# Turning attention weights by VectorE and transfers within SBUF in place of TensorE, in a stack of four graph layers

## The chip, the cores and the metric

The kernel runs on one core of one Trainium2 chip. The metric is the device time of one execution, in microseconds. Profiles are of one execution each.

Names used below: PE is TensorE, DVE is VectorE, ACT is ScalarE, POOL is GpSimd, SP is SyncE, whose queue issues all transfers. SBUF is the working memory of 128 partitions, and PSUM the memory that PE writes to.

## The reference

The input is 32 graphs of 512 nodes with 256 channels, and one adjacency matrix of 512x512 for all. Four layers follow each other; each is a graph attention whose output is added to its input and normalised. All is float32.

```python
# --- layer 0: one head of 256, additive
h = x @ W;  s1 = h @ a1;  s2 = h @ a2
e = leaky_relu(s1[:, :, None] + s2[:, None, :], 0.2)
att = softmax(where(adj > 0, e, NEG));  x = layernorm(x + elu(att @ h))
# --- layer 1: a transformer block, eight heads of 32, with softmax((q k^T)/sqrt(32)) masked, two
#     layer norms and a feed-forward part of 256; then x = layernorm(x + block(x))
# --- layer 2: four heads of 64, additive as layer 0, head by head; elu
# --- layer 3: e = leaky_relu((x W1) (x W2)^T), masked softmax, att @ (x W3), relu
```

The weights `att` of a head are computed with the query in the partition (128 queries a block, 512 keys in the row). The product `att @ h` sums over keys, and PE sums over partitions, so every block of weights has to be turned first.

## The kernel before

**Names.** The layers are called a (layer 0), b, c and d. `B` is 32 graphs, `N` 512 nodes, `P` 128, `NB` 4 blocks of 128 nodes, `F` 2 halves of a graph, `FB` 2 blocks in a half. `Gat` (L716) is the class for a and c, `Transformer` (L814) for b, `Bilinear` (L951) for d.

**The steps of an additive head** (`Gat.attend`, L741). PE spreads the target's score over all partitions as a row of 512 (L755). For each of four blocks, DVE adds the mask, writes a tile `t` of 128x512 and takes the row's maximum (`masked`, L637). ACT applies the leaky slope (L666) and the exponential with the sum of the row (L672), in place. Then `turn` (L543) turns each block: four PE transposes of 128x128 into one PSUM bank (L549), and a copy of 128x512 from the bank into the tile `pT`, on ACT (L492) or DVE (L494). Layer c multiplies two heads at a time by `weighted` (L554, matmuls L561), with the values as the stationary operand; layer a uses `rows_weighted` (L801, matmuls L807), with the turned weights as the stationary operand. `scaled` (L580) divides by the sums. Layers b and d use the same `turn`; b's scores come from L853, its mask and minimum from L867, its exponential from L874; d's scores come from L975.

**Counts.** A graph has 16 turned blocks in layer c, 4 in a, 32 in b and 4 in d, or 1792 blocks and 7168 transposes in all.

**Buffers.** A tile `t` is 2 KB a partition and there are 18; a `pT` holds half a graph's turned weights of one head, 4 KB, and there are 8. PSUM has 8 banks.

**What sets the order.** The program is a list of operations, each with the engines it may run on and a cost in microseconds (`Plan.op`, L107). `Plan.order` (L140) plays this list with these costs. At each free engine it picks the ready operation with the lowest key, made of the graph's number times `AGE`, the remaining path, and a table `URGENT` by engine and stage; up to `WINDOW` = 4 graphs are open at once. It also assigns every buffer slot and, where an operation may run on ACT or DVE (`copied`, L487), the engine. Its result is written out as a fixed order for each engine (L1062). At run time the engines keep that order and wait for each other by semaphores. SP's queue holds the loads of `x` and of its transpose (L340) and the stores (L1041), in that order too. The tables `AGE`, `URGENT` and `SWITCH_WEIGHT` are numbers written into the file.

Of the kernel before, what the change touches and what calls it, by code (L numbers as in the profile page):

```python
# [11 lines left out]
I32 = mybir.dt.int32  # L12
# [15 lines left out]
BUFS = dict(t=18, pT=8, x=6, xT=3, v=5, qk=4, y=5, e=2, n=2, nT=2, hT=2, oT=4, small=8)  # L28
# [11 lines left out]
AGE = {"PE": 51, "ACT": 138, "DVE": -107, "POOL": 461, "SP": 20}  # L40
URGENT = {
    "PE": {"a0": -417, "a1": 491, "a2": -867, "b0": -448, "b1": 197, "b2": 839, "c0": -557, "c1": -258, "c2": 203, "d0": -909, "d1": -511, "d2": -1186, "a3": 1287, "a4": 1218, "b3": -47, "b4": 169, "c3": 2234, "c4": 712},
    "ACT": {"a0": -671, "a1": 422, "a2": 770, "b0": 459, "b1": 253, "b2": 93, "c0": 729, "c1": 136, "c2": -360, "d0": 573, "d1": -523, "d2": -1234, "a3": 806, "a4": -162, "b3": 370, "b4": 340, "c3": 698, "c4": -390},
    "DVE": {"a0": -247, "a1": 1195, "a2": 496, "b0": 1368, "b1": 273, "b2": -132, "c0": -1160, "c1": 19, "c2": 666, "d0": -845, "d1": -1056, "d2": -1458, "a3": 1297, "a4": 438, "b3": -527, "b4": 175, "c3": 138, "c4": 1482},
    "POOL": {"a0": -896, "a1": -817, "a2": 582, "b0": 3, "b1": -713, "b2": 227, "c0": -148, "c1": -607, "c2": 1624, "d0": 582, "d1": 1022, "d2": -1512, "a3": -446, "a4": 431, "b3": 270, "b4": 1342, "c3": 708, "c4": 734},
    "SP": {},
# [6 lines left out]
SWITCH_WEIGHT = 661  # L53
# [45 lines left out]
class Plan:  # L99
# [7 lines left out]
    def op(self, where, issue, writes=(), reads=(), takes=(), lag=0.0, port=False, form="full"):  # L107
# [10 lines left out]
        for buf in takes:  # L118
            if not buf.users and buf.tag is not None:
                o.takes.append(buf)  # L120
                self.bufs.append(buf)
                buf.users.append(o)
# [170 lines left out]
def gnn_stack(  # L293
# [83 lines left out]
    def attention_weights(w, w_sb, a, H, D, name):  # L377
# [3 lines left out]
        for which, lo in enumerate((0, D)):  # L381
            av = buf("t", [P, D], f"{name}_a{which}")
            on_all(a[lo : lo + D], av)
            for k in range(NC):
                prod = buf("t", [P, H, D], f"{name}_prod{which}{k}")
# [14 lines left out]
    def mask():  # L400
        for i in range(NB):
            adj_sb = buf("t", [P, N], f"adj{i}", dtype=I32)
            load(adj_sb, lambda adj_sb=adj_sb: adj_sb[:], adj[block(i)])

            def issue(e, i=i, adj_sb=adj_sb):
                nc.vector.tensor_scalar(neg[:, i], adj_sb[:], 0.0, NEG, ALU.is_le, ALU.mult)

            op({DVE: 0.4}, issue, [(neg, i)], [adj_sb])

    def feed_forward_weights():  # L410


        b2_sb = buf("t", [P, C], "b2_sb")
# [32 lines left out]
    def bilinear_weights():  # L446
# [3 lines left out]
        for w, name in ((wa, "wa"), (wb, "wb")):  # L450
            w_sb = buf("t", [P, NC, C], f"{name}_sb")
            by_chunk(w, w_sb)
            wT = buf("t", [P, NC, C], f"{name}T", NC)
# [89 lines left out]
    def turn(t, pT, i, name):  # L543

        ps = bank([P, NB, P], name)

        def issue(e):
            for j in range(NB):
                nc.tensor.transpose(ps[:, j], t[:, block(j)], ident)  # L549

        op({PE: 0.44}, issue, [ps], [t], [pT])
        copied(N, lambda: pT[:, :, block(i)], lambda: ps[:], [(pT, i)], [ps])

    def weighted(pv, oT, pTs, v, lo, D, us):  # L554
# [3 lines left out]
        def issue(e):  # L558
            for j in range(NB):
                for h, pT in enumerate(pTs):  # L560
                    nc.tensor.matmul(  # L561
                        pv[h * D : (h + 1) * D], lhsT=v[:, j, lo + h * D : lo + (h + 1) * D],
                        rhs=pT[:, j], start=(j == 0), stop=(j == NB - 1), skip_group_check=True,
# [16 lines left out]
    def scaled(dst, cell, lo, ps, inv, D):  # L580


        def issue(e):
# [5 lines left out]
                inv[:].unsqueeze(3).to_broadcast([P, FB, n // D, D]),  # L589
# [43 lines left out]
    def masked(s, t, top, at, i):  # L633


        def issue(e):
            nc.vector.tensor_tensor_reduce(  # L637
                out=t[:], in0=s[:], in1=neg[:, i], scale=1.0, scalar=LOWEST, op0=ALU.add,
                op1=ALU.max, accum_out=top[(slice(None),) + at],
            )  # L640

        op({DVE: 0.61}, issue, [t, top], [s, (neg, i)])

    def leaky_softmax(ts, top, v, src, H, f, name):
# [3 lines left out]
        bias = tiny("bias", [P, FB, H], f"{name}_bias")  # L648
        total = tiny("total", [P, FB, H], f"{name}_total")
        inv = tiny("inv", [P, FB, H], f"{name}_inv")  # L650
        if src is not None:
            op(
                {DVE: 0.1},
                lambda e: nc.vector.tensor_tensor(top[:], top[:], v[:, part(f), src : src + H], ALU.add),
                [top], [(v, 2 * f), (v, 2 * f + 1)],
            )

        def negated(e):
            nc.scalar.activation(bias[:], top[:], AF.Prelu, alpha=SLOPE)
            nc.scalar.mul(bias[:], bias[:], -1.0)  # L660

        op({ACT: 0.3}, negated, [bias], [top])
        for (h, i), t in ts.items():

            def leaky(e, h=h, i=i, t=t):
                nc.scalar.activation(  # L666
                    t[:], t[:], AF.Prelu, alpha=SLOPE,
                    bias=0.0 if src is None else v[:, f * FB + i, src + h : src + h + 1],
                )

            def exp(e, h=h, i=i, t=t):
                nc.scalar.activation(  # L672
                    t[:], t[:], AF.Exp, bias=bias[:, i, h : h + 1], accum_out=total[:, i, h : h + 1]
                )

            op({ACT: 0.53 if src is None else 0.62}, leaky, [t], [] if src is None else [(v, f * FB + i)])
            op({ACT: 0.71}, exp, [t, total], [bias])
        pTs = []
        for h in range(H):
            pT = buf("pT", [P, NB, FN], f"{name}_pT{h}", FB)  # L680
            for i in range(FB):
                turn(ts[h, i], pT, i, f"{name}_tr{h}{i}")
            pTs.append(pT)
        op({DVE: 0.1}, lambda e: nc.vector.reciprocal(inv[:], total[:]), [inv], [total])
        return pTs, inv
# [30 lines left out]
    class Gat(Layer):  # L716
# [24 lines left out]
        def attend(self):  # L741
            H, D, name, v = self.H, C // self.H, self.name, self.v
            G = min(H, P // D) if H > 1 else 1
            for g in range(0, H, G):
                ts = {}
                for h in range(G):
                    dst = bank([P, N], f"{name}_dst{g}{h}")
                    for i in range(NB):
                        ts[h, i] = buf("t", [P, N], f"{name}_t{g}{h}{i}")
# [7 lines left out]
                    op({PE: 0.44}, issue, [dst], [v], [ts[h, i] for i in range(NB)])  # L757
                    if h == 0:
                        tops = [
                            tiny("top", [P, FB, G], f"{name}_top{g}{f}") for f in range(F)  # L760
                        ]
                    for i in range(NB):
                        masked(dst, ts[h, i], tops[i // FB], (i % FB, slice(h, h + 1)), i)
                for f in range(F):
                    plan.stage = name[0] + "3"
                    pTs, inv = leaky_softmax(
                        {(h, i): ts[h, f * FB + i] for h in range(G) for i in range(FB)},
                        tops[f], v, C + g, G, f, f"{name}_{g}_{f}",
                    )
                    y = self.part_y(f)  # L770
                    plan.stage = name[0] + "4"
                    if H > 1:
                        pv = bank([P, FN], f"{name}_pv{g}{f}")
                        oT = buf("oT", [P, 1, FN], f"{name}_oT{g}{f}")
                        weighted(pv, oT, pTs, v, g * D, D, 1.86)
                        copied(FN, lambda oT=oT: oT[:, 0], lambda pv=pv: pv[:], [oT], [pv])
                        ps = turned_back(oT, 1, y, f"{name}_{g}{f}")
                        op({DVE: 0.4}, scaled(y, 0, g * D, ps, inv, D), [y], [ps, inv])
                    else:
                        pv = bank([P, FB, C], f"{name}_pv{f}")  # L780
                        rows_weighted(pv, pTs[0], v, y)
                        op({DVE: 0.62}, scaled(y, 0, 0, pv, inv, C), [y], [pv, inv])
# [18 lines left out]
    def rows_weighted(pv, pT, v, y):  # L801
# [292 lines left out]
```

## Time and profile before

| | |
|---|---|
| time, median of 3 runs | 3526.16 us (3526.12 to 3527.19) |
| profiled execution, its own time | 3525.66 us |
| profiled execution, span from first to last instruction | 3523.9 us |
| granted TensorE clock | 0.999 |
| instructions | 68878 |
| HBM read, written | 38.21 MB, 16.78 MB |

How to read the lines below. A line of totals gives an engine's busy time, its share of the span and its instructions. PEld is the loading of the stationary operand, which overlaps PE. The chain is followed back from the last instruction, at each step to what released it or to the instruction before it on its engine. A line of a group gives source line, engine, operation, written and read tiles with shapes, the count, then busy time in us, the mean of one in ns, and the idle time of the engine just ahead of the group with what ended most of it. A float32 matmul leaves two records, a transpose one. Busy time of a group counts overlapping records once, so that busy time divided by the count is less than the mean of one.

### The profile page before, as it was taken

How to read it: one execution, taken by the hardware profiler on the slowest of the kernel's cores; microseconds unless marked ns; L12 is line 12 of the kernel's file. 1: busy time of each engine (PE TensorE's matmuls, PEld its weight loads, DVE VectorE, ACT ScalarE, POOL GpSimd, SP SyncE). 2: the span in 40 equal slices, each digit the busy share in tenths (PEclk: the TensorE clock that was granted, in tenths of full speed). 3: DMA queues.
4: the chain of work that ended last, by engine and by line, in shares of the span. 5: the costliest groups of instructions: out<-in, count | busy, mean ns of one | idle time of the engine just before them, and what ended most of it. 6: DMA issues, size and time to landing. Idle time of an engine off the chain costs nothing.

```text
span 3523.9 us, 68878 instructions
## 1 busy us (share of the span) xinstructions
PE 3501.5 (99%) x24728; PEld 2685.4 (76%) x24728; DVE 2973.8 (84%) x8792; ACT 2807.6 (80%) x6856; POOL 869.1 (25%) x840
## 2 busy tenths in 40 slices
PE   8999999999999999999999999999999999999999
PEld 7777777778777787877878778687787877878777
DVE  7789888888888888888888888888888888888886
ACT  6798877878788787887888878887788877888786
POOL 1222222222222222222222222222222222222322
PEclk9999999999999999999999999999999999999999
DMA  3000100001000010000100001000010000100000
GB/s 95 7 2 1 37 1 19 19 1 37 1 19 19 1 37 1 19 19 1 37 1 19 19 1 37 1 19 19 1 37 1 19 19 1 37 1 19 19 7 19
DMA packets 56918, 59.41 MB, mean 17 GB/s; under 512 B 3968, under 2 KB 55808, under 8 KB 56576
## 3 DMA queue, kind: packets, MB, share of 16 engines
q1 hardware_dynamic: 56576, 55.00, 4.9%
q8 instruction: 196, 3.21, 0.4%
q14 instruction: 146, 1.20, 0.1%
HBM read 38.21 MB, written 16.78 MB: 16 GB/s over the span
## 4 chain that ended last, share of the span: by engine, by line
PE 99%; DVE 1%; ACT 0%; DMA 0%; issue 0%; SPq 0%; POOLq 0%; POOL 0%; DVEq 0%
PE ps L549 23%; PE ps L561 13%; PE ps L520 13%; PE ps L807 12%; PE ps L535 10%; PE ps L853 8%; PE ps L733 7%; PE ps L975 6%; PE ps L505 3%; PE ps L755 2%; PE ps L575 2%; DMA xT<-in_x_T 0%; SPq L340 0%; DVE st L603 0%; DVE rstd L606 0%
## 5 line engine op out<-in xcount | busy, mean ns | idle before, releaser
L549 PEld LDWEIGHTS ps<-ident,t 128*128 128x128 f32 x7168 | 805.5, 141 | 178.4 <-issue 38.7
L549 PE MATMUL ps<-ident,t 128*128 128x128 f32 x7168 | 898.4, 274 | 1.0 <-ACT t L874 0.8
L874 ACT ACTIVATE t<-t,low 128x512 f32<-128x512 f32 x1024 | 734.8, 735 | 41.5 <-DVE low L867 41.5
L492 ACT COPY pT<-ps 128x512 f32<-128x512 f32 x1099 | 594.1, 593 | 119.9 <-PE ps L549 116.4
L867 DVE CUSTOM_DVE_ANT_0 t<-ps,neg 128x512 f32<-128x512 f32 x1024 | 649.0, 686 | 46.2 <-PE ps L853 43.6
L629 POOL TENSOR_TENSOR y<-y,x 128x512 f32<-128x512 f32 x256 | 330.0, 1290 | 1371.7 <-DVE y L586 493.3
L609 POOL TENSOR_TENSOR rstd<-rstd,mhalf 128x2 f32<-128x2 f32 x384 | 297.2, 774 | 1049.1 <-DVE rstd L606 934.3
L637 DVE CUSTOM_DVE_ANT_0 t<-ps,neg 128x512 f32<-128x512 f32 x768 | 492.3, 683 | 69.9 <-PE ps L975 59.4
L672 ACT ACTIVATE t<-t,bias 128x512 f32<-128x512 f32 x768 | 544.0, 709 | 0.4
L561 PE MATMUL ps<-pT,v 128*32 128x256 f32 (+1 forms) x6144 | 486.1, 382 | 0.0
L494 DVE COPY pT<-ps 128x512 f32<-128x512 f32 x693 | 451.3, 682 | 40.1 <-PE ps L549 37.8
L807 PE MATMUL ps<-v,pT 128*128 128x256 f32 x2048 | 465.5, 379 | 0.0
L666 ACT ACTIVATE t<-t,v 128x512 f32<-128x512 f32 x640 | 418.4, 715 | 32.5 <-DVE top L637 32.4
L561 PEld LDWEIGHTS ps<-pT,v 128*32 128x32 f32 (+1 forms) x6144 | 260.4, 118 | 208.1 <-issue 22.6
L807 PEld LDWEIGHTS ps<-v,pT 128*128 128x128 f32 x2048 | 378.5, 190 | 48.2 <-issue 2.3
L853 PE MATMUL ps<-qk,qk 32*128 32x512 f32 x2048 | 291.7, 639 | 0.0
L603 DVE BATCH_NORM_STATS2 st<-y 128x6 f32<-128x256 f32 x768 | 285.2, 413 | 4.5 <-POOL y L629 3.1
L975 PE MATMUL ps<-xT,qk 128*128 128x512 f32 x512 | 241.7, 596 | 0.0
L520 PE MATMUL ps<-xT,w_qkv_sb 128*128 128x256 f32 x1024 | 230.8, 379 | 0.0
L617 DVE TENSOR_SCALAR x<-y,mv,rstd 128x256 f32<-128x256 f32 x512 | 219.3, 474 | 3.7 <-POOL rstd L609 1.9
L874 ACT ACTIVATION_READ_ACCUMULATOR t<-t,low 128x1 f32 x1024 | 214.3, 209 | 0.0
L586 DVE TENSOR_TENSOR y<-ps,inv 128x512 f32<-128x512 f32 (+1 forms) x256 | 140.9, 551 | 83.9 <-PE ps L807 72.0
(84 smaller groups left out, 4630.4 us busy)
## 6 DMA issues: line engine op xcount, KB each, us to landing
xT<-in_x_T SPq DMA_DIRECT2D x64, 256.0 KB, 3.2
x<-in_x SPq DMA_DIRECT2D x32, 512.0 KB, 4.5
out<-x SPq DMA_DIRECT2D x64, 256.0 KB, 2.2
t<-in_adj SPq DMA_DIRECT2D x4, 256.0 KB, 6.8
w_qkv_sb<-in_L_gnn_w_qkv SPq DMA_DIRECT2D x1, 768.0 KB, 7.2
w_sb<-in_L_gnn_w SPq DMA_DIRECT2D x2, 256.0 KB, 5.8
t<-in_L_gnn_W SPq DMA_DIRECT2D x2, 256.0 KB, 2.8
w_sb<-in_L_gnn_W SPq DMA_DIRECT2D x1, 256.0 KB, 2.8
```

What stands on the lines that cost most here:

```text
L492: nc.scalar.copy(dst(), ps())
L494: nc.vector.tensor_copy(dst(), ps())
L520: nc.tensor.matmul(ps[:, c], lhsT=w[:, k, lo + c * P : lo + (c + 1) * P], rhs=xT[:, k, nlo : nlo + FN], start=(k == 0), stop=(k == NC - 1),)
L549: nc.tensor.transpose(ps[:, j], t[:, block(j)], ident)
L561: nc.tensor.matmul(pv[h * D : (h + 1) * D], lhsT=v[:, j, lo + h * D : lo + (h + 1) * D], rhs=pT[:, j], start=(j == 0), stop=(j == NB - 1), ...
L637: nc.vector.tensor_tensor_reduce(out=t[:], in0=s[:], in1=neg[:, i], scale=1.0, scalar=LOWEST, op0=ALU.add, op1=ALU.max, accum_out=top[(sli ...
L672: nc.scalar.activation(t[:], t[:], AF.Exp, bias=bias[:, i, h : h + 1], accum_out=total[:, i, h : h + 1])
L807: nc.tensor.matmul(pv[:, i], lhsT=pT[:, j, block(i)], rhs=v[:, j, 0:C], start=(j == 0), stop=(j == NB - 1),)
L853: nc.tensor.matmul(s[:], lhsT=q_sb[at, c, block(f * FB + i)], rhs=k_sb[at, c], start=True, stop=True,)
L867: nc.vector.tensor_tensor_reduce(out=t[:], in0=s[:], in1=neg[:, f * FB + i], scale=-1.0 / math.sqrt(D1), scalar=HIGHEST, op0=ALU.add, op1= ...
L874: nc.scalar.activation(t[:], t[:], AF.Exp, bias=low[:, i, h : h + 1], scale=-1.0, accum_out=total[:, i, h : h + 1],)
L975: nc.tensor.matmul(s[:], lhsT=hh[:, k, block(f * FB + i)], rhs=xT[:, k], start=(k == 0), stop=(k == NC - 1),)
```

## The change

Layers a and c no longer turn their weights on PE. A head's four blocks share one tile `tq` of 8 KB. After the exponential, DVE turns each block in place in squares of 32x32 (`nc.vector.transpose`, 128x512). Then 16 transfers within SBUF, issued from SP, bring the squares to their places in a tile `pq` of 8 KB: one for each pair of a source group and a destination group of 32 partitions, each with 16 runs of 128 bytes in each of 32 partitions, 64 KB in all. The products of both halves read `pq`, and wait for all 16 transfers. A head's bias, sums and reciprocals are formed for all 512 rows at once. Layers b and d still turn on PE, but use the same buffers of 8 KB: in b, a `tq` holds four heads of one block and a `pq` two heads of half a graph; in d, both hold all 512 rows. There are five of each. In b the tile of all four heads is taken as one. The counts of the other buffers change by one (`x` 6 to 5, `xT` 3 to 4, `qk` 4 to 5, `y` 5 to 6, `oT` 4 to 3).

The planner's numbers `AGE`, `URGENT` (which gains entries for SP and for the stages d3 and d4) and `SWITCH_WEIGHT` are replaced, so the order of the whole program differs. A scratch area for GpSimd's transfers is cut to 1024 bytes.

```diff
-BUFS = dict(t=18, pT=8, x=6, xT=3, v=5, qk=4, y=5, e=2, n=2, nT=2, hT=2, oT=4, small=8)
+BUFS = dict(x=5, xT=4, v=5, qk=5, y=6, e=2, n=2, nT=2, hT=2, oT=3, tq=5, pq=5, small=8)
...
-SWITCH_WEIGHT = 661
+SWITCH_WEIGHT = 53
+
+
+SQ = 32
+
+
+DMA_US = 0.45
+FLIP_US = 0.6
+
+
+BY_TRANSFERS = "ac"
...
             if not buf.users and buf.tag is not None:
                 o.takes.append(buf)
                 self.bufs.append(buf)
+            if not buf.users or buf.users[-1] is not o:
                 buf.users.append(o)
...
-    def turn(t, pT, i, name):
+    def turn(t, cell, pT, pcell, to, name):
 
         ps = bank([P, NB, P], name)
 
         def issue(e):
             for j in range(NB):
-                nc.tensor.transpose(ps[:, j], t[:, block(j)], ident)
-
-        op({PE: 0.44}, issue, [ps], [t], [pT])
-        copied(N, lambda: pT[:, :, block(i)], lambda: ps[:], [(pT, i)], [ps])
-
-    def weighted(pv, oT, pTs, v, lo, D, us):
+                nc.tensor.transpose(ps[:, j], t[:, cell, block(j)], ident)
+
+        op({PE: 0.44}, issue, [ps], [(t, cell)], [pT])
+        copied(N, to, lambda: ps[:], [(pT, pcell)], [ps])
...
+    def turned(t, pT, blocks, name):
+
+
+        if name[0] not in BY_TRANSFERS:
+            for i in blocks:
+                turn(
+                    t, i, pT, i, lambda i=i: pT[:, i * NB : (i + 1) * NB], f"{name}_tr{i}"
+                )
+            return
+
+        for i in blocks:
+            op({DVE: FLIP_US}, lambda e, i=i: nc.vector.transpose(t[:, i], t[:, i]), [(t, i)], [])
+
+        def squares():
+            return t[:].rearrange("p i (j n) -> p (i j) n", n=P)
+
+        for a in range(P // SQ):
+
+            def move(e, a=a):
+                here = slice(a * SQ, (a + 1) * SQ)
+                for b in range(P // SQ):
+                    there = slice(b * SQ, (b + 1) * SQ)
+                    nc.sync.dma_start(out=pT[there, :, here], in_=squares()[here, :, there])
+
+            op({SP: P // SQ * DMA_US}, move, [(pT, a)], [t], lag=3.0)
...
-        pTs = []
-        for h in range(H):
-            pT = buf("pT", [P, NB, FN], f"{name}_pT{h}", FB)
-            for i in range(FB):
-                turn(ts[h, i], pT, i, f"{name}_tr{h}{i}")
-            pTs.append(pT)
-        op({DVE: 0.1}, lambda e: nc.vector.reciprocal(inv[:], total[:]), [inv], [total])
-        return pTs, inv
...
-                ts = {}
+                total = tiny("total", [P, NB, G], f"{name}_total{g}", NB * G)
+                inv = tiny("inv", [P, NB, G], f"{name}_inv{g}")
+                pTs = []
                 for h in range(G):
+                    plan.stage = name[0] + "1"
                     dst = bank([P, N], f"{name}_dst{g}{h}")
-                    for i in range(NB):
-                        ts[h, i] = buf("t", [P, N], f"{name}_t{g}{h}{i}")
+                    t = buf("tq", [P, NB, N], f"{name}_t{g}{h}", NB)
+                    pT = buf("pq", [P, NB * NB, P], f"{name}_pT{g}{h}", NB)
+                    top = tiny("top", [P, NB], f"{name}_top{g}{h}", NB)
 
 
                     def issue(e, at=C + H + g + h, dst=dst):
@@ -754,32 +795,34 @@
                             column = v[:, j, at : at + 1].to_broadcast([P, P])
                             nc.tensor.transpose(dst[:, block(j)], column, ident)
 
-                    op({PE: 0.44}, issue, [dst], [v], [ts[h, i] for i in range(NB)])
-                    if h == 0:
-                        tops = [
-                            tiny("top", [P, FB, G], f"{name}_top{g}{f}") for f in range(F)
-                        ]
+                    op({PE: 0.44}, issue, [dst], [v], [t])
                     for i in range(NB):
-                        masked(dst, ts[h, i], tops[i // FB], (i % FB, slice(h, h + 1)), i)
+                        masked(dst, t, top, i)
+                    plan.stage = name[0] + "3"
+                    leaky_softmax(t, top, v, C + g + h, total, h, range(NB), f"{name}_{g}{h}")
+                    turned(t, pT, range(NB), f"{name}_{g}{h}")
+                    pTs.append(pT)
+                op({DVE: 0.1}, lambda e, a=inv, b=total: nc.vector.reciprocal(a[:], b[:]), [inv], [total])
                 for f in range(F):
-                    plan.stage = name[0] + "3"
-                    pTs, inv = leaky_softmax(
-                        {(h, i): ts[h, f * FB + i] for h in range(G) for i in range(FB)},
-                        tops[f], v, C + g, G, f, f"{name}_{g}_{f}",
-                    )
                     y = self.part_y(f)
                     plan.stage = name[0] + "4"
                     if H > 1:
                         pv = bank([P, FN], f"{name}_pv{g}{f}")
                         oT = buf("oT", [P, 1, FN], f"{name}_oT{g}{f}")
-                        weighted(pv, oT, pTs, v, g * D, D, 1.86)
+                        weighted(
+                            pv, oT, pTs,
+                            lambda h, j, f=f, pTs=pTs: pTs[h][:].rearrange(
+                                "p (i j) n -> p i j n", j=NB
+                            )[:, part(f), j],
+                            v, g * D, D, 1.86,
+                        )
                         copied(FN, lambda oT=oT: oT[:, 0], lambda pv=pv: pv[:], [oT], [pv])
                         ps = turned_back(oT, 1, y, f"{name}_{g}{f}")
-                        op({DVE: 0.4}, scaled(y, 0, g * D, ps, inv, D), [y], [ps, inv])
+                        op({DVE: 0.4}, scaled(y, f, g * D, ps, inv, D), [y], [ps, inv])
                     else:
                         pv = bank([P, FB, C], f"{name}_pv{f}")
-                        rows_weighted(pv, pTs[0], v, y)
-                        op({DVE: 0.62}, scaled(y, 0, 0, pv, inv, C), [y], [pv, inv])
+                        rows_weighted(pv, pTs[0], v, y, f)
...
-    def rows_weighted(pv, pT, v, y):
+    def rows_weighted(pv, pT, v, y, f):
 
         for i in range(FB):
 
             def issue(e, i=i):
                 for j in range(NB):
                     nc.tensor.matmul(
-                        pv[:, i], lhsT=pT[:, j, block(i)], rhs=v[:, j, 0:C],
+                        pv[:, i], lhsT=pT[:, (f * FB + i) * NB + j], rhs=v[:, j, 0:C],
                         start=(j == 0), stop=(j == NB - 1),
                     )
 
-            op({PE: 1.73}, issue, [pv], [(pT, i), v], [y])
+            reads = pT if y.name[0] in BY_TRANSFERS else (pT, f * FB + i)
+            op({PE: 1.73}, issue, [pv], [reads, v], [y])
...
+                    ts = [buf("tq", [P, Q, N], f"{name}_t{f}{c}{i}", Q) for i in range(FB)]
...
-                        buf("pT", [P, NB, FN], f"{name}_pT{f}{c}{q}", FB) for q in range(Q)
+                        buf("pq", [P, 2 * NB, FN], f"{name}_pT{f}{c}{k}", 2 * FB)
+                        for k in range(Q // 2)
...
+            t = buf("tq", [P, NB, N], f"{name}_t", NB)
+            pT = buf("pq", [P, NB * NB, P], f"{name}_pT", NB)
...
-    nc = bacc.Bacc("TRN2", target_bir_lowering=False, num_devices=1)
+    nc = bacc.Bacc("TRN2", target_bir_lowering=False, num_devices=1, dynamic_dma_scratch_size=1024)
...
```

`AGE` goes from {PE 51, ACT 138, DVE -107, POOL 461, SP 20} to {PE 102, ACT -120, DVE 53, POOL -74, SP 74}. In `leaky_softmax` the same operations are issued as before, for whole heads in a and c, without the turning at its end; `masked` writes a block of `tq`.

## The prediction

> **What bounds the kernel now.** I read the totals, then the chain that ended last, then the costliest groups, then stretches from the middle of the run.
>
> ```profile
> PE 3501.5 (99%) x24728; PEld 2685.4 (76%) x24728; DVE 2973.8 (84%) x8792; ACT 2807.6 (80%) x6856; POOL 869.1 (25%) x840
> ...
> PE 99%; DVE 1%; ACT 0%; DMA 0%; issue 0%; SPq 0%; POOLq 0%; POOL 0%; DVEq 0%
> PE ps L549 23%; PE ps L561 13%; PE ps L520 13%; PE ps L807 12%; PE ps L535 10%; PE ps L853 8%; PE ps L733 7%; PE ps L975 6%; PE ps L505 3%; PE ps L755 2%; PE ps L575 2%; DMA xT<-in_x_T 0%; SPq L340 0%; DVE st L603 0%; DVE rstd L606 0%
> ```
>
> A busy PE alone proves little, but here the chain lies on PE for 99%, and the largest link is the turning of the weights, L549. The stretches in the middle agree (columns: stretch, PE, PEld, DVE, ACT, POOL busy):
>
> ```profile
> 1400.00:1500.00 100.00, 100.00 (x700) 79.69 (x699) 85.47 (x258) 82.43 (x203) 22.80 (x22) 1.00 0.05 17
> 1500.00:1600.00 100.00, 100.00 (x712) 74.61 (x711) 83.90 (x242) 76.75 (x186) 28.79 (x27) 1.00 0.05 17
> ```
>
> PE has no gap; DVE and ACT have some 15 and 20 us free in each 100. The groups around the change:
>
> ```profile
> L549 PE MATMUL ps<-ident,t 128*128 128x128 f32 x7168 | 898.4, 274 | 1.0 <-ACT t L874 0.8
> ...
> L492 ACT COPY pT<-ps 128x512 f32<-128x512 f32 x1099 | 594.1, 593 | 119.9 <-PE ps L549 116.4
> L867 DVE CUSTOM_DVE_ANT_0 t<-ps,neg 128x512 f32<-128x512 f32 x1024 | 649.0, 686 | 46.2 <-PE ps L853 43.6
> ...
> L494 DVE COPY pT<-ps 128x512 f32<-128x512 f32 x693 | 451.3, 682 | 40.1 <-PE ps L549 37.8
> ```
>
> The mean of one turning, 274 ns, is no price, since PE's records overlap. The chain's view gives L549 22.7% of 3523.9 us: 800 us for 7168, or 111.6 ns each. DVE's records overlap too, as a stretch of its timeline shows (start, length):
>
> ```profile
> 1402.21 0.69 DVE L867 CUSTOM_DVE_ANT_0 t<-ps,neg 128x512 f32<-128x512 f32 x1
> 1402.83 0.08 DVE L867 DVE_READ_ACCUMULATOR2_ANT low<- 128x1 f32 x1
> 1402.83 0.69 DVE L867 CUSTOM_DVE_ANT_0 t<-ps,neg 128x512 f32<-128x512 f32 x1
> ```
>
> Packed, such a reduce costs 0.61 us, while its groups' busy time comes to 0.716 each. So DVE can take more work than 84% busy suggests. The transfers' queues:
>
> ```profile
> DMA packets 56918, 59.41 MB, mean 17 GB/s; under 512 B 3968, under 2 KB 55808, under 8 KB 56576
> ...
> q1 hardware_dynamic: 56576, 55.00, 4.9%
> ```
> ```profile
> 372.69 0.96 SPq L340 DMA_DIRECT2D xT<-in_x_T  x2
> 373.75 0.42 SPq L340 DMA_DIRECT2D x<-in_x  x1
> ```
>
> The DMA engines are idle for 95%; SP issues one transfer in about 0.5 us (two from 372.69 to 373.75).
>
> [...]
>
> **The change part by part.** *PE:* layers a and c turn 5 heads x 4 blocks x 4 squares in each of 32 graphs: 2560 matmuls go, 4608 stay. 2560 x 0.1116 = 286 us, all on the chain. The other matmuls keep their number and size. PE alone would end at a span of 3523.9 - 286 = 3238.
>
> *DVE and ACT:* I counted the built order of the changed kernel. 640 copies of 128x512 disappear, and the planner reassigns those that stay: DVE's copies of 512 columns fall from 944 to 557, ACT's from 1424 to 1134. DVE gains 640 turnings. Nearest row: L795 (128x512, SBUF to SBUF), 685 ns a record. [...] DVE: 2973.8 - 387 x 0.651 + 640 x 0.65, and +10 for small copies less reductions of smalls: 2974 - 252 + 416 + 10 - 10 = 3138 busy. Packed reduces take 1792 x (0.716 - 0.611) = 188 off, so about 2950 must fit into 3238: 91% [...]. ACT: 2807.6 - 290 x 0.54 - 30 = 2621, no bound. POOL keeps its 840 instructions.
>
> *Transfers:* each head adds 16 of 64 KB, 512 runs of 128 B: 2560 in all, 1.31 million packets, 81,920 per engine if all 16 share. Packet records of before: 4 B 8.9 ns (3713 of them), 256 B 18.2 ns, and over the whole queue 4.9% x 16 x 3523.9 / 56,576 = 48.8 ns for about 1 KB. Between the first two, 128 B is 13.6 ns: 32 x 13.6 = 0.44 us a transfer. Bounds: 0.29 and 1.56 us. I take SP's pace, 0.51. SP: 2560 x 0.51 = 1306 us, 40% of the span; engines 1114 us, 34%. Beside PE's work this costs nothing if it arrives in time.
>
> *Does it arrive?* A head's first transfer waits on SP for its fourth turning[...]. Behind these in SP's queue are the next graph's loads and the stores of this one; PE's L561 and L807 wait for the landing. In the changed order, priced by the steps above, PE has 31.2 us of work between the broadcast (L755) of layer c's fourth head and the matmul that needs it, 44 us for the first pair, 32.5 for layer a. The chain: four reduces 2.4, bias 0.5, four leaky and exp at 0.61 + 0.71 each 5.3, a turning 0.6, sixteen issues 8.2, landing 2.2 (the stores' median): 19.2. The third head's transfers start 4.0 us earlier and take 8.2, so 4.2 more: 23.4. Some 7.8 us remain for queueing on DVE and ACT. That is thin cover: it is gone when a transfer costs 0.51 + 7.8/32 = 0.75 us, and beyond that every 0.1 us costs 3.2 us a graph.
>
> *Buffers:* 18 of 2 KB and 8 of 4 KB become 5 and 5 of 8 KB. A graph takes 14 of each, so at 101 us a graph one may be held 36 us on average. Slots are fixed by the planner; a late reader delays the next writer. I cost this with the stall below.
>
> *Sum:* 3238 + 1.8 (time outside the span: 3525.66 - 3523.9) = 3240 against the profiled 3525.66; the median shown is 0.5 us above that. PE was idle for 22 us, 12 of them at the start. With DVE near 91% full, thin cover and coarser buffers I add 1.5 us of waits a graph, an estimate between nothing and 6: 48 us. Forecast 3288.
>
> **The rivals.** *VectorE becomes the bound.* For: 91% packed, 97% by records, and everything else passes through it. Against: ACT can take copies, and 15% were free. [...]
>
> *Transfers set the pace, slower than before.* Mechanism: 128-byte packets cost more than their bytes, so the fourth head of layer c reaches PE late in each graph. It decides at 9 us lost a graph (286/32): 0.75 + 9/32 = 1.03 us a transfer, 32 ns a packet. At the 48.8 ns of a 1 KB packet: 81,920 x 48.8 = 4000 us on each engine, and that is the time. For: nothing of before shows such traffic at length. Against: 18.2 ns at 256 B.
>
> *Buffers serialise.* If a buffer is held 39 us on average, a graph takes 14 x 39 / 5 = 109 us: 3500, the gain used up. That the turnings would not leave PE is excluded by the built order.
>
> **How the numbers follow.** Forecast (3240 to 3340) 0.55; VectorE (3340 to 3480) 0.20; transfers 0.17; buffers 0.08, split around no change. Faster by over 0.2%, about what a measurement can tell, 0.78; within it 0.03; slower 0.19. The range runs from PE's own floor, 3236, to 3500: outside it stay the transfers and a part of the buffers, 0.2. The cheap ends of turning and transfer change nothing below PE's floor.
>
> **What would show it.** After: L549's successor with 4608 matmuls near 515 us of the chain; PE still above 95% of the chain; StreamTranspose records near 0.65 us; packets of 128 B near 14 ns; SP issuing at about 0.5 us; PE's waits for DMA under 50 us. I am wrong if PE waits for pq transfers by several us in each graph, if packets take over 24 ns, if a turning takes over 1 us, or if the chain moves to DVE.

## The result, and the profile after

The changed kernel takes 3695.22 us (median of 4 runs, 3695.0 to 3706.84) against 3526.19 us (3526.12 to 3527.19) for the kernel before on the same chip: a ratio of 1.0487, 95% interval 1.0466 to 1.0507. The forecast was 3288. The profiled execution is the longest of the four, 3706.84 us, with a span of 3704.9 and a granted clock of 0.964 (0.966 to 0.968 in the others).

From the page of the kernel after: totals, the transfers' queue, the chain, and the groups that answer to those shown of before.

```profile
PE 3404.8 (92%) x22168; PEld 2484.9 (67%) x22168; DVE 3138.9 (85%) x8992; ACT 2644.6 (71%) x6464; POOL 860.9 (23%) x840
...
q1 hardware_dynamic: 1408256, 222.94, 31.9%
...
PE 58%; SPq 17%; DVE 13%; DMA 4%; ACT 4%; issue 4%; POOL 0%; DVEq 0%; POOLq 0%; ACTq 0%
...
L577 PE MATMUL ps<-pq,v 128*32 128x256 f32 (+1 forms) x6144 | 589.2, 407 | 168.0 <-DMA pq<-tq 164.9
...
L560 PE MATMUL ps<-ident,tq 128*128 128x128 f32 x4608 | 622.0, 277 | 15.1 <-ACT tq L906 9.0
...
L674 DVE STREAM_TRANSPOSE tq<-tq 128x512 f32<-128x512 f32 x640 | 432.1, 696 | 34.9 <-ACT tq L716 34.9
...
pq<-tq SPq DMA_DIRECT2D x2560, 64.0 KB, 2.1
```

The chain, 99% PE before, now has 17% on SP's queue. The products of layer c (L577) had no idle time ahead of them; now they have 168 us, and 165 of it ends with the landing of a `pq` transfer. SP's timeline shows what was late (start, length, line, count of issues in a row):

```profile
1864.54 10.67 SPq L685 DMA_DIRECT2D pq<-tq  x16
1876.84 2.26 SPq L1098 DMA_DIRECT2D out<-x  x2
1879.15 1.00 SPq L351 DMA_DIRECT2D xT<-in_x_T  x2
1880.26 48.05 SPq L685 DMA_DIRECT2D pq<-tq  x64
```

Four heads of 16 transfers stand in one unbroken row. It takes 48.05 us, 0.75 us an issue; two loads from HBM take 0.5 each beside it. The row ends at 1928. At 1915 PE comes to products of a head whose transfers end with the third quarter of the row (PE goes on at 1918.63; a transfer's last packet ends 1.75 us after its issue, so the issue that it waited for stands at 0.76 of the row):

```profile
1914.64 0.65 PE L577 MATMUL ps<-pq,v 128*64 128x256 f32 x2
1918.63 6.49 PE L577 MATMUL ps<-pq,v 128*64 128x256 f32 x30 [3.35 <-DMA pq<-tq]
```

PE begins two matmuls, then stands for 3.35 us. What follows is the second part of the loss, seen in stretches around this wait (stretch and length; busy time of PE, PEld, DVE, ACT and POOL; then the granted clock, the share of the DMA engines and GB/s):

```profile
1905.00:1915.00 10.00, 9.90 (x86) 6.01 (x84) 9.68 (x27) 8.76 (x24) 2.54 (x2) 1.00 0.57 96
1917.60:1924.40 6.80, 5.76 (x28) 3.75 (x29) 1.24 (x5) 2.08 (x6) 0.00 (x0) 0.50 0.54 90
1924.40:1934.00 9.60, 9.60 (x82) 6.94 (x82) 7.38 (x21) 6.03 (x14) 6.14 (x5) 1.00 0.32 54
```

For 6.8 us PE's clock is halved. The waits of 3.7 to 4.7 us between 1800 and 2100 (from one matmul's start to the next) each have such a stretch of 3.4 or 6.8 us; those of 1.4 to 1.8 us have none. In the 20 graphs of the steady part, as it is taken below, all 15 waits of more than 3.6 us have one, and 5 of the 35 between 1.2 and 3.6 us. Over the run these stretches come to 271 us in 45 pieces; before there were 8 us, at the very end. Of the 45, 44 are 3.41 us long or a multiple of that. The shortest wait that brings one on is not shown: two waits of 1.7 and 1.8 us have such a stretch here, and 12 of 20 waits of 2.9 us in the run with a new order below. The prediction had no such term.

To see where in the run the time lies, I took the 20 graphs between the 7th and the 27th store as the steady part. "Ends" is the span less 32 such periods: the filling and draining of the pipeline.

| kernel | period of a graph | PE busy a graph | half-rate clock a graph | ends | span |
|---|---|---|---|---|---|
| before | 109.19 | 109.19 | 0 | 30 | 3523.9 |
| after | 111.08 | 105.00 | 4.44 | 150 | 3704.9 |

The period became 1.9 us longer in place of 7.4 shorter ((3286 - 30) / 32 = 101.75 by the forecast), and the ends 120 us longer. Before, the last four stores are 168, 40, 25 and 24 us after one another; after, 112, 103, 84 and 80.

### The profile page after: what moved, and what is told of

Its sections match the earlier page's. It is cut to its first block, busy times and chain, and to the rows that moved or that the text cites. A ratio compares the mean times of both kernels' runs of the same rounds, so it can differ in the third digit from the quotient of the medians.

```text
span 3704.9 us, 66872 instructions
## 1 busy us (share of the span) xinstructions
PE 3404.8 (92%) x22168; PEld 2484.9 (67%) x22168; DVE 3138.9 (85%) x8992; ACT 2644.6 (71%) x6464; POOL 860.9 (23%) x840
## 4 chain that ended last, share of the span: by engine, by line
PE 58%; SPq 17%; DVE 13%; DMA 4%; ACT 4%; issue 4%; POOL 0%; DVEq 0%; POOLq 0%; ACTq 0%
SPq L685 17%; PE ps L577 12%; PE ps L560 10%; PE ps L531 8%; PE ps L850 6%; PE ps L1023 6%; PE ps L546 5%; PE ps L888 4%; DMA pq<-tq 3%; PE ps L770 3%; DVE tq L674 3%; DVE st L622 2%; PE ps L516 2%; DVE tq L656 2%; DVE y L1045 1%
## 5 line engine op out<-in xcount | busy, mean ns | idle before, releaser
L906 ACT ACTIVATE tq<-tq,low 128x512 f32<-128x512 f32 x1024 | 731.9, 719 | 171.0 <-DVE low L899 170.8
L577 PE MATMUL ps<-pq,v 128*32 128x256 f32 (+1 forms) x6144 | 589.2, 407 | 168.0 <-DMA pq<-tq 164.9
L899 DVE CUSTOM_DVE_ANT_0 tq<-ps,neg 128x512 f32<-128x512 f32 x1024 | 652.2, 683 | 26.0 <-PE ps L888 20.8
L560 PE MATMUL ps<-ident,tq 128*128 128x128 f32 x4608 | 622.0, 277 | 15.1 <-ACT tq L906 9.0
L560 PEld LDWEIGHTS ps<-ident,tq 128*128 128x128 f32 x4608 | 525.6, 141 | 144.8 <-ACT tq L906 52.8
L577 PEld LDWEIGHTS ps<-pq,v 128*32 128x32 f32 (+1 forms) x6144 | 313.3, 128 | 452.3 <-issue 214.6
L716 ACT ACTIVATE tq<-tq,bias 128x512 f32<-128x512 f32 x768 | 545.3, 713 | 1.1
L656 DVE CUSTOM_DVE_ANT_0 tq<-ps,neg 128x512 f32<-128x512 f32 x768 | 500.6, 682 | 30.1 <-PE ps L1023 25.5
L710 ACT ACTIVATE tq<-tq,v 128x512 f32<-128x512 f32 x640 | 425.0, 717 | 123.9 <-DVE top L656 122.1
L850 PE MATMUL ps<-v,pq 128*128 128x256 f32 x2048 | 466.5, 384 | 22.3 <-DMA pq<-tq 22.3
L674 DVE STREAM_TRANSPOSE tq<-tq 128x512 f32<-128x512 f32 x640 | 432.1, 696 | 34.9 <-ACT tq L716 34.9
L850 PEld LDWEIGHTS ps<-v,pq 128*128 128x128 f32 x2048 | 387.8, 192 | 87.6 <-issue 19.8
```

What stands on the lines that cost most here:

```text
L560: nc.tensor.transpose(ps[:, j], t[:, cell, block(j)], ident)
L577: nc.tensor.matmul(at, lhsT=v[:, j, lo + h * D : lo + (h + 1) * D], rhs=p, start=(j == 0), stop=(j == NB - 1), skip_group_check=True,)
L656: nc.vector.tensor_tensor_reduce(out=t[:, i], in0=s[:], in1=neg[:, i], scale=1.0, scalar=LOWEST, op0=ALU.add, op1=ALU.max, accum_out=top[: ...
L674: op({DVE: FLIP_US}, lambda e, i=i: nc.vector.transpose(t[:, i], t[:, i]), [(t, i)], [])
L716: nc.scalar.activation(t[:, i], t[:, i], AF.Exp, bias=bias[:, i : i + 1], accum_out=total[:, i, at : at + 1],)
L850: nc.tensor.matmul(pv[:, i], lhsT=pT[:, (f * FB + i) * NB + j], rhs=v[:, j, 0:C], start=(j == 0), stop=(j == NB - 1),)
```

## The experiments

The first theory was: SP issues these transfers at 0.67 to 0.75 us, while the order was laid out with 0.45 (`DMA_US`) and the prediction with 0.51, so weights arrive late. Rivals were VectorE's load, the 128-byte packets, and the coarse buffers. Ratios are to the kernel before, with 95% intervals.

**Four whole transfers a head.** Order and work of the changed kernel, but the sixteen transfers become four of 256 KB. Products use misplaced weights.

```diff
-                for b in range(P // SQ):
-                    there = slice(b * SQ, (b + 1) * SQ)
-                    nc.sync.dma_start(out=pT[there, :, here], in_=squares()[here, :, there])
+                nc.sync.dma_start(out=pT[:, a * NB : (a + 1) * NB], in_=squares()[:, a * NB : (a + 1) * NB])
```

> The changed kernel in its own order, but each head's 16 transfers of 64 KB are replaced by 4 of 256 KB in which every partition keeps its 2 KB runs (the squares are left in the wrong places; flips, buffers, order and bytes are the same). Theory 1, the pace of issue on SP (0.67 to 0.75 us a transfer where the order was made for 0.45): PE's waits for pq shrink from 229 us to under 40, the half-rate stretches of the clock nearly go (mean clock 0.99), 3300 to 3450 us. Theory 2, the order and the buffers of 8 KB leave PE without work whatever the transfers cost: 3600 us or more, waits of PE moved from pq to ACT and DVE. Theory 3, VectorE is the bound: 3600 or more with DVE busy over 90%.

Measured: 3445.42 us, ratio 0.9771 (0.9755 to 0.9787). What is left of PE's waits at L577 for `pq` (total, times, longest):

```profile
PE ps L577 <- DMA pq<-tq: 7.6, 2, 6.8
```

They fall from 165 to 7.6 us, no half-rate stretch remains in the steady part, the period is 104.03 us. The transfers' manner is worth 250 us. But this edit changes their number, their form and, as came out later, the moment when the first can start.

**Pace by form.** A kernel with no attention at all issues rows of transfers within SBUF, each row in another form.

```diff
+nc.sync.dma_start(out=dst[q[b], k[h], q[a]], in_=src[q[a], k[h], q[b]])
+nc.sync.dma_start(out=dst[q[b], 16 * h : 16 * h + 8, q[a]], in_=src[q[a], 16 * h : 16 * h + 8, q[b]])
+nc.sync.dma_start(out=dst[q[b], :, q[a]], in_=src[q[a], :, q[b]])
...
+nc.sync.dma_start(out=dst[q[a], 4 * h : 4 * h + 4], in_=src[q[a], 4 * h : 4 * h + 4])
...
+nc.sync.dma_start(out=dst[:, 4 * h : 4 * h + 4, q[a]], in_=src[:, 4 * h : 4 * h + 4, q[a]])
+nc.sync.dma_start(out=dst[:, h], in_=src[:, h])
+nc.sync.dma_start(out=flat[q[b], k[h], q[a]], in_=src[q[b], k[h], q[a]])
```

In this order: the change's form, 16 runs of 128 bytes in 32 partitions (L34); 8 runs (L38); 32 runs, 128 KB (L41); one run of 2 KB (L48); four runs of 128 bytes in 128 partitions (L51); one run of 512 bytes in 128 partitions (L53); the change's form without a change of partition (L57).

> No attention at all: rows of x are loaded, and one tile is moved within SBUF by eight series of transfers, each series on its own source line, then stored. Series: 32 of the change's form (32 partitions, 16 runs of 128 B), 32 with 8 runs, 16 with 32 runs, 32 with 4 runs, 32 of 32 partitions with one run of 2 KB, 32 of 128 partitions with 4 runs of 128 B, 32 of 128 partitions with one run of 512 B, and 32 of the change's form that stay in their partitions. If SP's pace is a fixed cost of an issue, all series run at 0.6 to 0.7 us; if it grows with the descriptors, the series with 8 and 4 runs run at about 0.5 us or less and the one with 32 runs at 1 us or more; if it is the shifted partitions, only the last series is faster.

SP's timeline of this kernel:

```profile
6.96 21.59 SPq L34 DMA_DIRECT2D dst<-src  x32
28.59 20.91 SPq L38 DMA_DIRECT2D dst<-src  x32
49.55 11.89 SPq L41 DMA_DIRECT2D dst<-src  x16
...
82.18 20.22 SPq L48 DMA_DIRECT2D dst<-src  x32
102.44 21.87 SPq L51 DMA_DIRECT2D dst<-src  x32
124.36 20.77 SPq L53 DMA_DIRECT2D dst<-src  x32
145.18 21.54 SPq L57 DMA_DIRECT2D flat<-src  x32
```

An issue costs 0.675, 0.653, 0.743, 0.632, 0.683, 0.649 and 0.673 us: nearly the same for one run as for sixteen, and only 0.07 more for twice the bytes. Crossing partitions costs nothing here (0.675 against 0.673). So the price on this queue is nearly one per transfer, 0.63 to 0.68 us from 16 to 64 KB, and 0.51 was the price of another kind of transfer.

**No flips.** As the run with four whole transfers, and the 640 turnings on DVE are left out too, so neither half of the turning is computed.

```diff
-            op({DVE: FLIP_US}, lambda e, i=i: nc.vector.transpose(t[:, i], t[:, i]), [(t, i)], [])
+            op({DVE: FLIP_US}, lambda e: None, [(t, i)], [])
```

> As e1_four_whole (4 whole transfers a head), and the 640 turnings of 32x32 squares on VectorE are left out too, in the same order; so neither half of the turning is computed in layers a and c. If VectorE's load is what remains of the loss after the issues are cheap (theory 3), the time falls from 3445 us by at least half of the 640 x 0.6 = 384 us of VectorE, to 3260 or less, near PE's own floor of 3240. If the written-out order and the buffers hold PE (theory 2), it stays above 3380. In between, both have a part.

Measured: 3431.16 us, ratio 0.9731 (0.9716 to 0.9745). DVE's busy time falls by 355 us, from 3122.9 to 2767.8, and the time by 14. With the transfers in time, VectorE is not the bound.

**A new order at the true pace.** All work is done. `DMA_US` is 0.72, with new numbers `AGE`, `URGENT`, `SWITCH_WEIGHT` and slightly other buffers (xT 3, y 8, e 3, oT 2).

```diff
-DMA_US = 0.45
+DMA_US = 0.72
```

> The changed kernel with all its work, whose order is planned with 0.72 us a transfer in place of 0.45, with tables AGE, URGENT and SWITCH_WEIGHT chosen anew for that and x, xT, y, e and oT buffers shifted by up to two within the same space. Theory 1 (the order places PE's matmuls before the transfers can have landed): PE's waits for pq fall from 229 us to under 80, the clock is back above 0.985, 3430 to 3560 us. Theory 2' (the transfers' latency cannot be covered with five buffers of 8 KB whatever the order): 3650 or more.

Measured: 3552.96 us, ratio 1.0076 (1.0059 to 1.0093): 142 us better than the changed kernel, still above before. PE waits 18.6 us at L577 for `pq`, as expected, but the clock is 0.979 to 0.981, not above 0.985; the period is 107.94, with 2.39 us at half rate, and the ends 91. PE's largest wait is now another, layer b's turnings behind their exponentials on ACT:

```profile
PE ps L560 <- ACT tq L906: 68.4, 34, 2.3
```

It was 9.0 us. Knowing the pace recovers a part; in this order the waits stand elsewhere.

**Layer c alone by transfers.** Layer a turns on PE again (64 transfers a graph in place of 80), with an order laid out for it at 0.72 (y 5, nT 3).

```diff
-BY_TRANSFERS = "ac"
+BY_TRANSFERS = "c"
-DMA_US = 0.45
+DMA_US = 0.72
```

> Only layer c is turned by VectorE and transfers (2048 of the 2560 PE transposes go, 229 us of PE), layer a goes back to PE; order planned with 0.72 us a transfer and tables chosen anew. Theory 1 expects a time below before, 3400 to 3500 us, since SP's work falls by a fifth and VectorE's by 128 turnings. Theory 2' expects no gain: 3550 or more.

Measured: 3470.15 us, ratio 0.9842 (0.9827 to 0.9857). It does all the work and takes 1.6% less than the kernel before and 6.1% less than the changed one. Period 104.31, no half-rate clock in the steady part, ends 130.

**None by transfers.** Both layers turn on PE, but with the 8 KB buffers and a new order.

```diff
-BY_TRANSFERS = "ac"
+BY_TRANSFERS = ""
```

> No transfers at all: both layers turn on PE as before, but with the buffers of 8 KB and the whole-head operations of the changed kernel, tables chosen anew for this list. If the coarser buffers by themselves cost PE its cover (theory 2), 3600 us or more; if they do not, within 1.5% of before, 3480 to 3580.

Measured: 3555.1 us, ratio 1.0082 (1.0067 to 1.0097). PE is busy for 99% again. Buffers of 8 KB together with another order cost 29 us here; they don't explain 169.

**Sixteen, and eight, whole transfers a head.** These were to separate the number of issues from their form: 16 of 512 bytes in each of 128 partitions, or 8 of 1 KB. The squares stay misplaced. The diff shows the first; the second steps by 2 and takes `b : b + 2`.

```diff
-                for b in range(P // SQ):
-                    there = slice(b * SQ, (b + 1) * SQ)
-                    nc.sync.dma_start(out=pT[there, :, here], in_=squares()[here, :, there])
+                for b in range(a * NB, (a + 1) * NB, 1):
+                    nc.sync.dma_start(out=pT[:, b : b + 1], in_=squares()[:, b : b + 1])
```

> The order of the changed kernel, and as many transfers: sixteen a head from the same queue, but each of 128 partitions by one run of 512 bytes, so the packets are four times longer, four times fewer, and nothing crosses partitions. The squares stay where the flip left them, so the products are taken with misplaced weights. Theory (the pace at which SP issues is what comes too late, 0.65 to 0.69 us a transfer in the run of paces whatever the form): within 1% of the changed kernel, 3660 to 3710 us, with PE's waits for pq ahead of L577 near 165 us. Rival (the packets of 128 bytes, 1.31 million, delay the landing or the engines): as with four transfers a head, 3440 to 3480 us.

> The order of the changed kernel, with eight transfers a head of 128 KB, 128 partitions by one run of 1 KB; the squares stay misplaced. By the pace of the run of paces a head then takes 8 x 0.65 to 0.75 = 5.2 to 6 us of SP, below the 16 x 0.45 = 7.2 us with which the order was laid out. Theory (what costs is lateness against that layout): as good as four transfers a head, 3440 to 3465 us, with PE's waits for pq near 10 us. Rival (each issue costs in itself, in proportion): halfway between four and sixteen on a line through 3445 at 4 and 3695 at 16, that is 3528 us.

Measured: 3453.52 us, ratio 0.9793 (0.9778 to 0.9808), and 3442.48, ratio 0.9764 (0.9747 to 0.978). The theory of the bare pace missed the first: as many issues, at nearly the same pace, and 242 us less. From SP's timeline of the sixteen:

```profile
1830.28 11.38 SPq L684 DMA_DIRECT2D pq<-tq  x16
...
1851.83 44.08 SPq L684 DMA_DIRECT2D pq<-tq  x64
```

A head's sixteen take as long as before, but they start elsewhere. I set the issues against the head's fourth flip in the 20 steady graphs (medians of the first of five heads, in us; the last issue counted to its end):

| kernel | fourth flip to first issue | first to last issue | fourth flip to last issue |
|---|---|---|---|
| after | 0.06 | 11.0 | 11.0 |
| sixteen whole | -3.8 | 11.0 | 7.2 |
| eight whole | -4.5 | 7.1 | 2.6 |
| four whole | -4.2 | 4.9 | 0.6 |

A transfer of whole blocks reads one block and starts with that block's flip. A transfer of the change reads 32 partitions of all four blocks, so nothing moves before the fourth flip. That was in the diff. The prediction had the fourth flip in its chain; the first theory, of the pace alone, did not use it.

**Sixteen whole, fourth block first.** The same transfers, put behind the fourth flip again by their order alone.

```diff
-        for a in range(P // SQ):
+        for a in reversed(range(P // SQ)):
```

> The run of sixteen whole transfers a head (3453.5 us) missed what the pace of issue predicted, though its sixteen took as long from first to last as in the changed kernel, 10.9 against 11.0 us. In its trace they begin 3.7 to 5.5 us before the head's fourth flip has ended, since such a transfer reads one block alone; in the changed kernel each transfer reads all four blocks and the first begins after the fourth flip. Here the same sixteen whole transfers are issued with the fourth block first, so that all stand behind the fourth flip again; size of packets, partitions and number are as in that run, the squares misplaced. Theory (what costs is that 16 issues at 0.67 us follow the fourth flip): back to the changed kernel, 3650 to 3700 us, first issue 0.1 us after the flip where SP is free, waits for pq near 165 us. Rival (packets of 128 bytes or the shift between partitions cost it): 3445 to 3465 us, as before.

Measured: 3559.77 us, ratio 1.0095 (1.008 to 1.011), between both expectations. By this route the distance splits into 106 us (3559.8 - 3453.5) for standing behind the fourth flip, and 135 us (3695.2 - 3559.8) for the form. SP, PE and the stretch after the wait in this kernel:

```profile
1912.24 46.93 SPq L684 DMA_DIRECT2D pq<-tq  x64
```
```profile
1945.44 0.65 PE L577 MATMUL ps<-pq,v 128*64 128x256 f32 x2
1947.10 3.15 PE L577 MATMUL ps<-pq,v 128*64 128x256 f32 x22 [1.02 <-DMA pq<-tq]
```
```profile
1946.00:1956.00 10.00, 8.98 (x67) 6.51 (x70) 7.04 (x20) 6.47 (x16) 3.10 (x3) 1.00 0.31 89
```

The row of 64 is 1.1 us shorter than in the changed kernel, and a transfer's last packet ends 1.60 us after its issue in place of 1.75. The wait at the same place is 1.02 us in place of 3.35, and no half-rate stretch follows: these take 0.34 us a graph against 4.44. So 1.3 us of lateness go with a period of 106.70 in place of 111.08. Of those 4.4 us, 2.9 are idle time of PE (3.15 a graph here against 6.08), and 1.5 are longer busy time, which fits the clock: 4.1 us fewer at half rate are at most 2 us of work. How 1.3 us of lateness become 2.9 us of waits is not shown; that lateness feeds back into the next graph's flips is a guess. Which trait of the form makes the row longer, the runs of 128 bytes or the source over four blocks, is not separated in the full kernel. The run of paces points to the runs: 0.683 us an issue for four of 128 bytes (L51), 0.649 for one of 512 (L53), both in 128 partitions and from one block; over 64 issues that is 2.2 us.

**A second queue.** All work and the order of the changed kernel; every second transfer goes out from POOL's queue (shown), or from ACT's (`nc.scalar`).

```diff
-                    nc.sync.dma_start(out=pT[there, :, here], in_=squares()[here, :, there])
+                    queue = nc.sync if b % 2 == 0 else nc.gpsimd
+                    queue.dma_start(out=pT[there, :, here], in_=squares()[here, :, there])
```

> The changed kernel, all its work and its order, but every second transfer of a head is issued from POOL's queue, at the place where the planner put it; POOL is busy for 23% otherwise. What an issue takes there no trace of this case shows. Theory (sixteen issues in one queue after the fourth flip are too long): eight in each queue side by side, 5.5 us from first to last if POOL issues as fast as SP, and 3440 to 3490 us; at over 1.2 us an issue nothing is gained. Rival (packets of 128 bytes): their number and form are unchanged, so 3650 to 3700 us.

> As the run with POOL's queue, with ACT's queue in place of POOL's: ACT is busy for 71%, and its list has the leaky slopes and exponentials of other heads behind the transfers, which then wait for the flips too. Theory: the sixteen land as early as with two queues (5.5 us from first to last), but ACT is held for 8 x 0.6 us in each of 160 heads, 770 us beside its 2645 busy of some 3500: about 3460 to 3600 us, better than the changed kernel, worse than with POOL's queue. Rival (packets of 128 bytes): 3650 us or more.

Measured: 5059.82 us with POOL, ratio 1.4345 (1.4323 to 1.4366); 3672.42 with ACT, ratio 1.0421 (1.0404 to 1.0439). POOL's timeline shows why the first is no answer:

```profile
2014.12 0.65 POOL L686 DMA_DIRECT2D pq<-tq  x1 [1.99 <-issue]
2016.96 0.65 POOL L686 DMA_DIRECT2D pq<-tq  x1 [2.19 <-issue]
2019.32 0.65 POOL L686 DMA_DIRECT2D pq<-tq  x1 [1.70 <-issue]
2021.70 0.65 POOL L686 DMA_DIRECT2D pq<-tq  x1 [1.73 <-issue]
```

POOL issues one in about 2.5 us. Its scratch area is the one cut to 1024 bytes; whether a larger one is faster was not run. With ACT the transfers are in time: PE's waits at L577 for `pq` fall from 165 to 19 us and the half-rate stretches to 0.85 us a graph. The time is in the range of the rival, 3650 us or more, but not for its reason, since the packets are the same and the waits for them are gone. The issuing is shared out, with a median of 0.64 us an issue on SP and 0.62 on ACT; from issue to landing the median is 2.2 us, against 2.1 in the changed kernel. ACT, though, now stands behind flips and issues, and PE's turnings of b wait for it:

```profile
PE ps L560 <- ACT tq L907: 65.7, 92, 4.0
```

That was 9.0 us. L577 waits 32.6 us for copies on ACT, and L591 30.7. The period is 111.21 against 111.08: other waits took the place of the first.

**Layer c alone, ordered again.** As the version with layer c alone above, with loads counted 1.4 us longer until they land, nT 2 and hT 3 buffers, and new numbers for the order. The diff shows the loads.

```diff
-        op({SP: 0.1 + kb * 0.003}, issue, [dst if cell is None else (dst, cell)], [], lag=2.0)
+        op({SP: 0.1 + kb * 0.003}, issue, [dst if cell is None else (dst, cell)], [], lag=3.4)
```

> Layer c alone by transfers, as in the earlier run of that (3470.2 us), with the order laid out again: a load counts 1.4 us longer until it lands (3.4 in place of 2.0 us after its issue, as the median of 3.5 us in the profile suggests), DMA_US 0.72 and new numbers AGE, URGENT and SWITCH_WEIGHT. Theory (what is left of waits are transfers later than the order has them): PE's waits ahead of L770 for xT stay under 5 us in all and the time goes to 3445 to 3465 us. Rival (the order has nothing left to give, PE's own busy time of 3343 us and the ends of the run set it): 3465 to 3480 us.

Measured: 3475.44 us, ratio 0.9855 (0.9839 to 0.9872): no gain over 0.9842, as the rival had it. PE waits 2.8 us for the loads of xT at L770, as hoped, but in the version above it had been only 2.1 us (in the changed kernel 36.2): what the edit was to remove was not there. The period is 104.37 and the ends 134.

## Why the prediction was wrong

The forecast's span was 3286, the profiled one 3704.9. The prediction named waits of PE for `pq` of several us in each graph as a sign of being wrong, and the trace has them: 165 us at L577, 5.2 a graph. By its own steps:

*PE, "286 us, all on the chain":* right in count, too large in size. The matmuls fell from 24728 to 22168 as said. In the steady part of the run with sixteen whole transfers, where waits are few, PE is busy for 98% of 104.04, 102.2 us a graph, against 109.2 before: 7.0 a graph or 223 us in 32, 63 less than forecast. From one matmul's start to the next, the turnings that stay take 121 ns each in that part, against 112 before, so one price for all of them was too simple. The order differs too; in the run with none by transfers, which has another order and all 7168 turnings, they take 113, so the order alone need not do it. Why the turnings that stay cost more is open.

*DVE, ACT and POOL:* right. DVE 3138.9 us busy against 3138, a flip 0.675 against 0.65, which was the author's estimate, ACT 2645 against 2621; POOL's 840 instructions took 860.9 against 869.1 before. The rival that made VectorE the bound fell with the run without flips.

*Transfers, "I take SP's pace, 0.51":* this step failed first. The packets were as forecast, or cheaper: 12.0 ns for 128 bytes against 13.6. (A packet of 512 bytes took 27.3 ns in the runs with sixteen whole transfers; at 12.0 the smaller one moves at 57% of its rate.) But SP's steady step in the changed kernel is 0.672 us and the row's mean 0.75, since 0.51 came from two loads from HBM and was carried to transfers within SBUF.

*"Does it arrive?":* failed with it. The prediction gave 0.75 us a transfer as the price at which the cover is gone, counting 32 transfers in the queue. The trace has 0.75 and rows of 64, whose end is 64 x (0.75 - 0.51) = 15 us later than at the counted pace. The sixteen do wait for the fourth flip, as the prediction said, but it priced them at 8.2 us and they took 11.0. The runs show that the pace costs where nothing can start ahead of the fourth flip: whole transfers, sixteen a head, cost 106 us more behind it than ahead of it, and the change's form 135 more again.

*"1.5 us of waits a graph":* failed. From the run with sixteen whole transfers (104.04) to the changed kernel (111.08) lie 7.0 us a graph, 225 us in all, 4.3 of them idle time of PE (6.08 against 1.82) and 2.8 longer busy time (105.00 against 102.22), for which the halved clock, which the prediction lacked, is the cause in sight. Without lateness 104.04 - 102.2 = 1.8 us remain, near the 1.5.

*The ends of the run:* no step at all; the floor of 3238 carried over the 30 us of before. They became 150. With transfers in time the same order still has 110 to 119, so of the 120 some 85 belong to how this order fills and drains, and some 35 come with lateness. The clock is in both: outside the 20 steady graphs the runs with four, eight and sixteen whole transfers have 79 to 86 us at half rate, where the kernel before has 6, so up to 40 of the 85 (half of that length, an estimate) can be the clock. Why this order drains graph after graph I did not test.

These add up: 63 for PE, 10 for the other waits (32 x (1.8 - 1.5)), 225 for lateness, 120 for the ends, 418 in all; 3704.9 - 3286 is 419.

*Rivals.* "Transfers set the pace" was right in place, layer c's products, and wrong in price. It asked for 32 ns a packet or 1.03 us a transfer; 12.0 ns and 0.75 us were enough: the rows are of 64, the waits halve PE's clock as well, and the ends were charged too. "Buffers serialise" fell with the run that has the buffers and no transfers, and with the three runs of whole transfers, which have the same buffers.

## What to carry to other kernels

Take the issue pace of a transfer from a transfer of the same kind (here 0.75 us in a row within SBUF, where loads from HBM had given 0.51), multiply it by the longest row in the queue (64 here), and place it behind the last producer that the first transfer reads. Sixteen transfers a head were harmless here where each could start with its own piece of the source (3453.5 us, against 3445.4 with four), and costly where all stood behind the whole (3559.8). When PE has no slack, look for a halved clock at its waits and price it with them: in the steady part of the changed kernel all 15 waits of more than 3.6 us had it, and 5 of the 35 between 1.2 and 3.6. Count the filling and draining of the pipeline as a term of its own (30 us before, 150 after).

## What the hardware showed that I had not expected

In the run of paces an issue within SBUF from SP took 0.63 to 0.68 us for every form of 16 to 64 KB tried, and 0.74 for 128 KB, against 0.5 for a load of 256 KB from HBM in the kernels before and after. The same transfer issued from POOL took about 2.5 us, with its scratch area at 1024 bytes. In the 20 steady graphs of the changed kernel, every wait of more than 3.6 us between the starts of two matmuls (15 of them) came with 3.4 or 6.8 us at half the clock; so did 12 of 20 waits of 2.9 us in the run with a new order. A packet of 128 bytes took 12.0 ns in the changed kernel, one of 512 bytes 27.3 in the runs with sixteen whole transfers.
